# Two heads of layer 0 side by side on TensorE, with the softmax sums added up on GpSimd

## The chip, the cores and the metric

The kernel runs on one core of a Trainium2 chip. A core has five engines that each work through a queue of their own in order: TensorE (PE; its weight loads are shown as PEld), VectorE (DVE), ScalarE (ACT), GpSimd (POOL) and SyncE (SP, which here issues DMAs). The metric is the device time of one execution in microseconds (us). Three runs of the kernel before gave 4607.11, 4602.47 and 4614.23 us, a median of 4607.11 us.

## The reference

Four layers are applied one after the other to four images of 32 x 32 pixels with 384 channels; every layer adds its result to its input. Only layer 0 is touched by the change. It is attention with six heads of 64 channels, in which each head's keys and values are sampled at moved positions and a sampled table of relative positions is added to the logits:

```python
k = (xs @ w_k + b_k).reshape(Bq, n, HEADS, HC)
v = (xs @ w_v + b_v).reshape(Bq, n, HEADS, HC)
attn = jnp.einsum('bmhc,bnhc->bhmn', qh, k) * scale
bias = _bilinear_sample(rpe_img, disp)
bias = bias.reshape(Bq, G, n, n, GH).transpose(0, 1, 4, 2, 3).reshape(Bq, HEADS, n, n)
attn = jax.nn.softmax(attn + bias, axis=-1)
out = jnp.einsum('bhmn,bnhc->bmhc', attn, v).reshape(Bq, Hq, Wq, NC)
return out @ w_out + b_out
```

Here n is 1024 (pixels), HEADS is 6 and HC is 64. So an image has six 1024 x 1024 logit matrices. Layers 1 to 3 (a second attention with twelve heads, a box filter, and a local attention) stay as they are.

## The kernel before, in words

All arithmetic is in float32. A channel chunk is 128 channels on 128 partitions, so three chunks (k = 0 to 2) hold the 384 channels, and each chunk holds two heads of 64 channels. Pixels are taken in eight blocks of 128 keys (j) and in two halves of 512 queries (q).

**Two lanes.** `Front` runs layer 0, `Trunk` runs layers 1 to 3. Layer 0 of image 0 runs alone, with a schedule of its own (`heads0`, L897 and after). Layer 0 of images 1, 2 and 3 is a generator that is advanced beside layers 1 to 3 of the image before it: each `yield w` of a lane states a share of the lane's work, and `Net.layer3` moves the front on until it is a little ahead of the trunk. That mixes the emission of the two lanes. The framework then reorders instructions on each engine within what the data and the buffers allow, so the order on an engine is its own and not that of the source; once built, each engine's order is fixed and a waiting instruction holds up those behind it.

**The stage around the change.** For each head h and query half q, `head0` (L815 to L895) does the following. For each j it has GpSimd gather a window of the position table (`win`, L830, an indirect DMA, four buffers), ScalarE and VectorE interpolate it (L842 and L847 on ScalarE, L843 and L848 on VectorE) into a logits tile `lg` of 128 keys x 512 queries (13 buffers), TensorE makes keys x queries in a PSUM bank (L851), and VectorE adds that to the logits (L852) and keeps a running maximum (L855, L857). The keys of one head lie in a tile `kz` of 128 partitions in which the other head's 64 rows are zero, so that the multiplication can run over the whole chunk. Then the maximum is turned on TensorE (L864), reduced (L868), spread over the partitions through a diagonal made on GpSimd (L870), a product with ones (L872) and a copy (L876). Last, for each j, VectorE subtracts it (L883), ScalarE takes the exponential (L884) and TensorE does two products of 64 output rows each (L886): the head's values, and a block of ones whose result is the softmax sum. Results and sums share one PSUM bank. `over_sums` (L1111) divides after each pair of heads: the sums go to DRAM and back for the reciprocals, which return spread over the partitions as two `inv` tiles.

**The trunk beside it.** In a pair of layer 1 heads (`pair`, six an image), a step j has TensorE make two logit tiles of two PSUM banks each (L1509), ScalarE take their exponentials (L1517), TensorE make the weights (transposes L1534, products L1539 of a tile `sg` that GpSimd scales at L1492) and VectorE multiply (L1546). Four products for the next pair's sums (L1382), their maximum on VectorE (L1390) and their exponentials on ScalarE (L1391) run in the same step, and so does the product with the values (L1481).

**PSUM.** Two tiles of two banks (`big`) and four tiles of one bank (`bank`) take all eight banks. Before, the front's stage uses only `bank`; the trunk's logits and sums go through `big`.

**DMA queues.** SP issues most loads and stores, among them the keys (L813) and the sums (L894). GpSimd's queue holds the window gathers L830, the scaling L1492 and the diagonal L870.

Of the kernel before, what the change touches and what calls it, by code (L numbers as in the profile page):

```python
# [26 lines left out]
P = 128  # L27
# [45 lines left out]
class Net:  # L73
# [132 lines left out]
    def scratch(self):  # L206
# [13 lines left out]
        self.k0 = dram("k0", [C, N])  # L220
        self.gcd = dram("gcd", [C, M1])
# [204 lines left out]
class Front(Lane):  # L426


    def layer0(self, b):
        nc, v = self.nc, self.nc.vector  # L430
        with self.scope("l0"):
# [3 lines left out]
            self.kz = [self.wt([P, N], f"kz{r}") for r in range(2)]  # L435
            for r in range(2):
                nc.gpsimd.memset(self.kz[r][GC * (1 - r) : GC * (2 - r), :], 0.0)
            self.va = self.wt([P, NJ, C], "va")
            self.f = self.wt([P, 2, 2, NJ * G], "bias_f")
            self.widx = self.wt([P, 2, NJ * G], "widx", 1, I32)  # L440
            if b == 0:

                self.side = "left"
                with self.scope("l0f"):
                    self.side = "right"
                    self.heads = self.heads0(self.work)
                    with self.scope("l0a"):
                        yield from self.inputs0(b)
                    yield from self.heads
                    self.side = "left"  # L450
                    yield from self.outputs0(b)
                    self.side = "right"
                return
            with self.scope("l0a"):
                yield from self.inputs0(b)
            with self.scope("l0b"):
                self.load_keys(0)
                for h in range(G):
                    if h + 1 < G:
                        self.load_keys(h + 1)  # L460
                    for q in range(2):
                        yield from self.head0(h, q)
                    if h % 2:
                        yield from self.over_sums(h // 2)
# [166 lines left out]
    def inputs0(self, b):  # L631
# [145 lines left out]
        va, bv = self.va, self.rows[:, R_BV0 : R_BV0 + C]  # L777
# [3 lines left out]
        def value(j):  # L781
            v.tensor_tensor(va[:, j, :], self.dense_n(xsT, w, j), bv, ALU.add)
# [32 lines left out]
    def head0(self, h, q):  # L815

        nc, v = self.nc, self.nc.vector
        f, kz, va = self.f, self.kz[h % 2], self.va
        k, r0 = h // 2, (h % 2) * GC
        rows = slice(r0, r0 + GC)  # L820
        other = slice(GC - r0, 2 * GC - r0)
        HH, HN = HW // 2, N // 2
        both = self.qpad[:, k, 1 + HH * q : 1 + HH * (q + 1), 1 : 1 + HW]
        queries = both[rows]
        logits = []
        rmax = self.wt([P, HN], "rmax", 2)
        for j in range(NJ):
            c = j * G + h
            win = self.wt([P, (HH + 1) * WROW], "win", 4)
            nc.gpsimd.indirect_dma_start(  # L830
                out=win,
                out_offset=None,
                in_=self.strips[:, :],
                in_offset=bass.IndirectOffsetOnAxis(
                    ap=self.widx[:, q, c : c + 1], axis=0
                ),
            )
            wv = win.rearrange("p (r c) -> p r c", c=WROW)
            sc = lambda i, t: f[:, i, t, c : c + 1]

            z = self.wt([P, HH, HW + 1], "z", 3)
            nc.scalar.activation(z, wv[:, 0:HH, 0 : HW + 1], AF.Copy, scale=sc(1, 1))  # L842
            v.scalar_tensor_tensor(  # L843
                z, wv[:, 1 : HH + 1, 0 : HW + 1], sc(0, 1), z, ALU.mult, ALU.add
            )
            lg = self.wt([P, HH, HW], "lg", 13)
            nc.scalar.activation(lg, z[:, :, 0:HW], AF.Copy, scale=sc(1, 0))  # L847
            v.scalar_tensor_tensor(lg, z[:, :, 1 : HW + 1], sc(0, 0), lg, ALU.mult, ALU.add)  # L848
            lf = lg.rearrange("p y x -> p (y x)")
            ps = self.bank()  # L850
            nc.tensor.matmul(ps, kz[:, j * P : (j + 1) * P], both, start=True, stop=True)  # L851
            v.tensor_tensor(lf, ps, lf, ALU.add)  # L852
            logits.append(lf)
            if j == 1:
                v.tensor_tensor(rmax, logits[0], lf, ALU.max)  # L855
            elif j > 1:
                v.tensor_tensor(rmax, rmax, lf, ALU.max)  # L857
            yield 3


        NI = HN // P
        ps = self.bank()
        for i in range(NI):
            nc.tensor.transpose(  # L864
                ps[:, i * P : (i + 1) * P], rmax[:, i * P : (i + 1) * P], self.ident
            )
        top = self.wt([P, NI], "top", 2)
        v.tensor_reduce(top, ps.rearrange("p (i n) -> p i n", i=NI), AX.X, ALU.max)  # L868
        diag = self.wt([P, NI, P], "diag", 1)
        nc.gpsimd.tensor_tensor(diag, bc(self.ident, 1, NI), bc(top, 2, P), ALU.mult)  # L870
        ps = self.bank()
        nc.tensor.matmul(  # L872
            ps, self.ones, diag.rearrange("p i n -> p (i n)"), start=True, stop=True
        )
        tb = self.wt([P, HN], "tb", 2)
        nc.scalar.copy(tb, ps)  # L876
        yield 3


        po = self.bank()  # L880
        for j in range(NJ):
            lf = logits[j]
            v.tensor_tensor(lf, lf, tb, ALU.subtract)  # L883
            nc.scalar.activation(lf, lf, AF.Exp)  # L884
            for out, w in ((rows, va[:, j, h * GC : (h + 1) * GC]), (other, self.ones[:, 0:GC])):
                nc.tensor.matmul(po[out, :], w, lf, start=j == 0, stop=j == NJ - 1)  # L886
            if j % 2:
                yield 2

        nc.scalar.copy(queries, po[rows, :].rearrange("p (y x) -> p y x", y=HH))  # L890
        o0 = other.start
        den = logits[0][o0 : o0 + 1, :]
# [1034 lines left out]
```

## Time and profile before

| what | value |
|---|---|
| median of the three runs | 4607.11 us |
| span of the profiled execution (first to last instruction) | 4578.1 us |
| median less span | 29.0 us |
| TensorE busy | 4150.6 us, 91% of the span |
| VectorE busy | 3138.6 us, 69% |
| ScalarE busy | 2303.6 us, 50% |
| GpSimd busy | 972.6 us, 21% |
| mean granted TensorE clock | 0.948 of full speed |

The profile gives no other time for its execution than the span; what lies around it is taken as the 29.0 us between that and the median. A group in the profile has one line per source line, engine, operation and tile: how many records, their busy time together, the mean of one, and the idle time before them with what ended it. A float32 product of 512 columns leaves two records on TensorE, so 288 instructions show as 576. Overlapping records are counted once in busy time. In a timeline the first two columns are the start and the length in us; "x8" merges eight records.

### The profile page before, as it was taken

Reading aid. Unit: us, or ns where it says so; the run is one execution under the profiler, and the core shown is the slowest. Engines: PE = TensorE matmul, PEld = TensorE weight load, DVE = VectorE, ACT = ScalarE, POOL = GpSimd, SP = SyncE. Lnnn points to the kernel's source line nnn. Section 1 sums busy time; section 2 is a strip of 40 time slices with the busy share of each in tenths; the row PEclk is TensorE's granted clock in tenths of the full one; section 3 lists DMA queues with packets and bytes.
Section 4 is the critical chain, followed back from the end, with each engine's and each line's share of the span. In section 5 each row is a group of like instructions: output and inputs, shape, how many; then the busy total and the mean of one; then the engine's idle time right before and its main releaser. Section 6 shows DMA issues by size and latency. Waiting matters only on the chain.

```text
span 4578.1 us, 47313 instructions
## 1 busy us (share of the span) xinstructions
PE 4150.6 (91%) x15896; PEld 1795.0 (39%) x15896; DVE 3138.6 (69%) x5909; ACT 2303.6 (50%) x3633; POOL 972.6 (21%) x994
## 2 busy tenths in 40 slices
PE   5699889999999898999999989899999998999998
PEld 2333334333334443433333444343333335344444
DVE  4599466878787628687878744678786884566654
ACT  2266334667664314465666422456665641555632
POOL 1644123212111104211212110522120211000000
PEclk8799989999999898999999989899999998999998
DMA  6444234212121245321212134432121213311011
GB/s 139 150 144 129 79 125 123 64 52 84 51 59 55 86 114 164 93 55 39 84 50 79 38 105 125 135 103 66 45 71 36 72 38 123 105 32 27 20 41 42
DMA packets 232852, 371.01 MB, mean 81 GB/s; under 512 B 117763, under 2 KB 165728, under 8 KB 232608
## 3 DMA queue, kind: packets, MB, share of 16 engines
q1 hardware_dynamic: 180568, 201.26, 15.4%
q0 software_dynamic: 39936, 145.53, 10.8%
q10 hardware_dynamic: 12104, 21.19, 1.4%
q8 instruction: 126, 2.06, 0.2%
q14 instruction: 118, 0.97, 0.1%
HBM read 287.90 MB, written 80.27 MB: 80 GB/s over the span
## 4 chain that ended last, share of the span: by engine, by line
PE 56%; DVE 14%; ACT 7%; issue 5%; DMA 4%; POOL 2%; SPq 0%; ACTq 0%; DVEq 0%; POOLq 0%
PE bank L1539 13%; PE big L1509 5%; PE big L1382 4%; PE bank L851 4%; PE big L403 4%; PE bank L886 4%; PE bank L417 4%; PE bank L1534 3%; PE bank L1481 3%; DVE nmax L1390 2%; DVE e L1546 2%; PE bank L1219 2%; PE big L666 2%; PE big L1664 1%; POOL gat L738 1%
## 5 line engine op out<-in xcount | busy, mean ns | idle before, releaser
L1539 PE MATMUL bank<-whole,sg 128*128 128x512 f32 (+3 forms) x2304 | 852.5, 505 | 7.0 <-POOL sg L1492 7.0
L1546 DVE SCALAR_TENSOR_TENSOR e<-bank,gam,e 128x512 f32<-128x512 f32 x768 | 561.9, 747 | 349.2 <-PE bank L1539 226.7
L1391 ACT ACTIVATE big<-big,nmax 128x1024 f32<-128x1024 f32 x384 | 417.6, 1087 | 322.3 <-DVE nmax L1390 322.1
L1517 ACT ACTIVATE e<-big 128x1024 f32<-128x1024 f32 x384 | 379.7, 1019 | 363.2 <-PE big L1509 362.1
L1539 PEld LDWEIGHTS bank<-whole,sg 128*128 128x128 f32 x2304 | 403.4, 197 | 369.6 <-issue 281.6
L1390 DVE TENSOR_REDUCE nmax<-big 128x1 f32<-128x1024 f32 x384 | 454.5, 1219 | 76.4 <-PE big L1382 75.9
L830 POOL DMA_INDIRECT win<-strips,widx x288 | 316.2, 1098 | 658.0 <-DVE z L843 391.8
L1492 POOL TENSOR_SCALAR sg<-whole,gam 128x512 f32<-128x512 f32 x192 | 143.7, 750 | 1442.6 <-PE bank L1539 1019.6
L1509 PE MATMUL big<-qa,ka 64*128 64x512 f32 x1536 | 417.8, 630 | 9.7 <-ACT big L1391 9.5
L1382 PE MATMUL big<-k,q 32*128 32x512 f32 x1536 | 327.7, 674 | 82.2 <-ACT big L1391 45.2
L738 POOL DMA_INDIRECT gat<-pairs,sidx x192 | 209.2, 1090 | 378.8 <-DVE ix_gt L519 217.4
L851 PE MATMUL bank<-qpad,kz 128*128 128x512 f32 x576 | 278.8, 613 | 9.4 <-ACT gf L1551 9.4
L886 PE MATMUL bank<-lg,va 128*64 128x512 f32 x576 | 265.6, 605 | 15.0 <-ACT lg L884 14.9
L886 PE MATMUL bank<-lg,ones 128*64 128x512 f32 x576 | 265.0, 605 | 0.0
L848 DVE SCALAR_TENSOR_TENSOR lg<-z,bias_f,lg 128x512 f32<-128x512 f32 x288 | 213.7, 759 | 47.4 <-ACT lg L847 45.7
L1509 PEld LDWEIGHTS big<-qa,ka 64*128 64x128 f32 x1536 | 135.7, 188 | 256.3 <-issue 124.3
L842 ACT ACTIVATE z<-win,bias_f 128x528 f32<-128x528 f32 x288 | 202.9, 735 | 55.4 <-DVE lg L848 34.4
L852 DVE TENSOR_TENSOR lg<-bank,lg 128x512 f32<-128x512 f32 x288 | 192.9, 685 | 49.4 <-PE bank L851 48.1
L883 DVE TENSOR_TENSOR lg<-lg,tb 128x512 f32<-128x512 f32 x288 | 191.5, 710 | 46.9 <-ACT tb L876 46.9
L843 DVE SCALAR_TENSOR_TENSOR z<-win,bias_f,z 128x528 f32<-128x528 f32 x288 | 215.5, 772 | 11.3 <-ACT z L842 9.8
L1481 PE MATMUL bank<-e,vs 128*32 128x512 f32 x1536 | 206.7, 604 | 3.9 <-DVE vs L1475 3.9
L847 ACT ACTIVATE lg<-z,bias_f 128x512 f32<-128x512 f32 x288 | 200.0, 716 | 12.0 <-PE bank L886 6.1
(314 smaller groups left out, 6620.8 us busy)
## 6 DMA issues: line engine op xcount, KB each, us to landing
pairs<-xn SPq DMA_DIRECT2D x64, 192.0 KB
q<-qd SPq DMA_DIRECT2D x48, 256.0 KB
w<-in_gmat SPq DMA_DIRECT2D x16, 576.0 KB
w<-in_w_off SPq DMA_DIRECT2D x12, 576.0 KB
w<-in_Wqkv SPq DMA_DIRECT2D x12, 576.0 KB
a<-in_x SPq DMA_DIRECT2D x16, 384.0 KB
x<-a ACTq DMA_DIRECT2D x4, 1536.0 KB
res<-x SPq DMA_DIRECT2D x12, 512.0 KB
```

Of the source, the lines that this page charges most:

```text
L738: nc.gpsimd.indirect_dma_start(out=gat[:, g].rearrange("p l c -> p (l c)"), out_offset=None, in_=pairs[:, :], in_offset=bass.IndirectOffse ...
L830: nc.gpsimd.indirect_dma_start(out=win, out_offset=None, in_=self.strips[:, :], in_offset=bass.IndirectOffsetOnAxis(ap=self.widx[:, q, c : ...
L851: nc.tensor.matmul(ps, kz[:, j * P : (j + 1) * P], both, start=True, stop=True)
L886: nc.tensor.matmul(po[out, :], w, lf, start=j == 0, stop=j == NJ - 1)
L1382: nc.tensor.matmul(ps[r][:, h * 512 : (h + 1) * 512], self.q4[rows, i * P : (i + 1) * P], self.k4[rows, 0:512], start=True, stop=True,)
L1390: v.tensor_reduce(nmax[:, r, i : i + 1], ps[r], AX.X, ALU.max, negate=True)
L1391: nc.scalar.activation(ps[r], ps[r], AF.Exp, bias=nmax[:, r, i : i + 1], accum_out=den[:, r, i : i + 1],)
L1481: nc.tensor.matmul(av[r0 : r0 + HD1, :], vs[:, r, :], es[h][:, r, :], start=j == 0, stop=j == NJ - 1,)
L1509: nc.tensor.matmul(ps[:, r, :], ka[rows, j * P : (j + 1) * P], qa[rows, cols], start=True, stop=True,)
L1517: nc.scalar.activation(e, ps, AF.Exp)
L1539: nc.tensor.matmul(ps[:, (mid - i0) * P :], sg[:, r, m, :], sim[:, h, r, m, (mid - i0) * P :], start=m == 0, stop=m == 1,)
L1546: v.scalar_tensor_tensor(e[:, r, :], ps, self.gam[:, 1:2], e[:, r, :], ALU.add, ALU.mult, accum_out=tot[:, r, h : h + 1],)
```

## The change

In images 1 to 3 the two heads of a chunk are now one unit (`two_heads`, six an image, in place of twelve calls of `head0`).

- The keys of a chunk are one tile of 128 partitions (`keys`, one buffer), 64 partitions a head; the two products of a j use 64 partitions each and write the two halves of a `big` tile. `kz` stays in image 0 alone.
- The values are written to a DRAM tensor `v0` (L782 before wrote them into `va` in SBUF) and loaded per chunk (`vals`, one buffer).
- Logits tiles are 128 x 1024 (two heads), nine buffers, so the additions, maxima, subtractions and exponentials are half as many and twice as wide. The interpolation keeps its size.
- The two products with the values write 64 partitions each of one bank. The product with ones in every j is gone: GpSimd adds up the exponential tiles (seven additions of 128 x 1024 a unit), and two products with ones follow at the end of the unit.
- The turned maxima and the product that spreads them go through `big` tiles; the diagonal is made in two parts.
- The `inv` tiles use the tag `z` (three buffers) in place of `lg`; the layer 1 tile `y` uses the tag `sg`.

```diff
+    def pair_keys(self, k):
+        t = self.wt([P, N], "keys")
+        self.nc.sync.dma_start(t, self.k0[k * P : (k + 1) * P, :])
+        return t
+    def pair_values(self, k):
+        t = self.wt([P, NJ, P], "vals")
+        self.nc.sync.dma_start(
+            t, self.v0[:, k * P : (k + 1) * P].rearrange("(j p) c -> p j c", p=P)
+        )
+        return t
-    def head0(self, h, q):
+    def two_heads(self, k, q):
...
         for j in range(NJ):
-            ps = self.bank()
-            nc.tensor.matmul(ps, kz[:, j * P : (j + 1) * P], both, start=True, stop=True)
-            v.tensor_tensor(lf, ps, lf, ALU.add)
+            lg = self.wt([P, 2, HN], "lg", 9)
+            ps = self.big()
+            for r in range(2):
+                nc.tensor.matmul(
+                    ps[:, r * HN : (r + 1) * HN],
+                    keys[half(r), j * P : (j + 1) * P],
+                    queries[half(r)],
+                    start=True,
+                    stop=True,
+                )
...
+            v.tensor_tensor(flat(lg), ps, flat(lg), ALU.add)
...
         po = self.bank()
+        acc = self.wt([P, 2, HN], "rmax", 2)
         for j in range(NJ):
-            v.tensor_tensor(lf, lf, tb, ALU.subtract)
-            nc.scalar.activation(lf, lf, AF.Exp)
-            for out, w in ((rows, va[:, j, h * GC : (h + 1) * GC]), (other, self.ones[:, 0:GC])):
-                nc.tensor.matmul(po[out, :], w, lf, start=j == 0, stop=j == NJ - 1)
+            lg = logits[j]
+            v.tensor_tensor(flat(lg), flat(lg), tb, ALU.subtract)
+            nc.scalar.activation(flat(lg), flat(lg), AF.Exp)
+            for r in range(2):
+                nc.tensor.matmul(
+                    po[half(r), :], vals[:, j, half(r)], lg[:, r], start=j == 0, stop=j == NJ - 1
+                )
+            if j:
+                first = logits[0] if j == 1 else acc
+                nc.gpsimd.tensor_tensor(flat(acc), flat(first), flat(lg), ALU.add)
...
+        ps = self.bank()
+        for r in range(2):
+            nc.tensor.matmul(
+                ps[half(r), :], self.ones[:, 0:GC], acc[:, r], start=True, stop=True
+            )
...
-            inv = self.wt([P, HH, HW], "lg", 13)
+            inv = self.wt([P, HH, HW], "z", 3)
```

The steps that the units state with `yield` add up to 76 a unit, as two calls of `head0` did.

## The prediction

> **What bounds the kernel now.** I first looked at busy time by engine: TensorE is busy 91% of the span. Then I asked where the changed lines run. They lie between 820 and 3769 us, in three stretches, one for each of images 1 to 3, in which layer 0 of an image shares the core with layers 1 and 2 of the image before. The view of busy time by stretch gives these stretches, and then one pair of layer 1 heads with the front beside it (975 to 1098) and one without (4124 to 4204):
>
> ```profile
> core 0: us, PE busy (x) PEld busy (x) DVE busy (x) ACT busy (x) POOL busy (x), PEclk, DMA share, GB/s
> 820.00:1541.00 721.00, 676.66 (x2632) 272.17 (x2631) 575.24 (x1097) 441.04 (x685) 136.51 (x136) 0.98 0.20 56
> 1933.00:2654.00 721.00, 676.86 (x2633) 272.17 (x2632) 575.83 (x1097) 441.41 (x685) 136.39 (x136) 0.98 0.20 56
> 3045.00:3769.00 724.00, 678.92 (x2636) 273.95 (x2635) 576.78 (x1097) 441.43 (x686) 137.30 (x137) 0.98 0.19 56
> ...
> 975.00:1098.00 123.00, 113.77 (x473) 45.05 (x469) 94.57 (x188) 77.59 (x124) 19.39 (x21) 1.00 0.17 47
> ...
> 4124.00:4204.00 80.00, 77.87 (x364) 33.46 (x363) 50.05 (x116) 48.20 (x76) 5.53 (x8) 1.00 0.12 28
> ```
>
> In each stretch TensorE is 94% busy (676.7 of 721), VectorE 80% (575.2), ScalarE 61%, GpSimd 19%. TensorE is the bound, and VectorE is not far behind. The front costs a pair 43 us (123 less 80): 36 us of TensorE and 44.5 us of VectorE.
>
> The groups show what the change takes from TensorE, and the rows of which VectorE's new operations are made:
>
> ```profile
> L851 PE MATMUL bank<-qpad,kz 128*128 128x512 f32 x576 | 278.8, 613 | 9.4 <-ACT gf L1551 9.4
> L886 PE MATMUL bank<-lg,va 128*64 128x512 f32 x576 | 265.6, 605 | 15.0 <-ACT lg L884 14.9
> L886 PE MATMUL bank<-lg,ones 128*64 128x512 f32 x576 | 265.0, 605 | 0.0
> L852 DVE TENSOR_TENSOR lg<-bank,lg 128x512 f32<-128x512 f32 x288 | 192.9, 685 | 49.4 <-PE bank L851 48.1
> L883 DVE TENSOR_TENSOR lg<-lg,tb 128x512 f32<-128x512 f32 x288 | 191.5, 710 | 46.9 <-ACT tb L876 46.9
> ```
>
> Mean durations on TensorE overlap, so starts must be compared. TensorE's timeline:
>
> ```profile
> 1179.69 0.59 PE L886 MATMUL bank<-lg,va 128*64 128x512 f32 x1
> 1179.69 0.59 PE L886 MATMUL bank<-lg,ones 128*64 128x512 f32 x1
> 1180.12 0.59 PE L886 MATMUL bank<-lg,va 128*64 128x512 f32 x1
> ...
> 1199.82 1.99 PE L851 MATMUL bank<-qpad,kz 128*128 128x512 f32 x4
> 1201.74 1.99 PE L1509 MATMUL big<-qa,ka 64*128 64x512 f32 x8
> 1203.66 1.09 PE L1534 MATMUL bank<-ident,gf 128*128 128x128 f32 x8
> ```
>
> The two 64-column products of L886 start together, and the next two 0.43 us later: they already run side by side, so one head's values and sums cost 2 x 0.43 = 0.86 us a block. Two products of L851 take 1.92 us, 0.96 each. L1509, 64 rows deep like the new keys product, gets four products into the same 1.92 us: they run in pairs, 0.96 a pair.
>
> **The change, part by part** (per image, a third of the whole; six units, 96 head blocks, 48 new blocks of two heads).
>
> *TensorE.* Keys: L851 is 278.8 / 3 = 92.9 us; after, 48 x 0.96 = 46.1. Saved 46.8. Values: 96 x 0.86 = 82.6; after, 48 x 0.86 = 41.3. Saved 41.3. Added: the two products with ones, 6 x 0.86 = 5.2. Turning and spreading the maximum keeps its count (8 transposes and 2 products a unit). So 676.7 becomes 593.8, 249 us less over three images.
>
> *VectorE.* The row nearest to a 128x1024 operation is L1691 at 1.23 us (both inputs in SBUF), or L1684 at 1.22 (one in PSUM). Two narrow ones cost 1.34 (192.9 / 144), 1.33 (191.5 / 144) and 1.37 (maximum, 0.687 each). 48 x (0.12 + 0.10) + 42 x 0.14 = 16.4 saved: 575.2 becomes 559. ScalarE saves about 10 and stays far from a bound.
>
> *GpSimd.* It gets 42 additions of 128x1024. The nearest row is L1686, a 128x1024 addition of 2.408 us: 101 us, so 136.5 becomes 238 of 721. That alone is no bound. [...] The trace has one clean meeting of the two:
>
> ```profile
> 1525.43 1.22 DVE L1684 SCALAR_TENSOR_TENSOR dn<-big,sq 128x1024 f32<-128x1024 f32 x1
> 1526.57 4.16 DVE L883 TENSOR_TENSOR lg<-lg,tb 128x512 f32<-128x512 f32 x5
> ...
> 1525.31 2.45 POOL L1686 TENSOR_TENSOR whole<-sq,whole 128x1024 f32<-128x1024 f32 x1 [3.74 <-ACT sq L1680]
> ```
>
> L1684, with one input in PSUM, ran its usual 1.22 us under the addition. The five subtractions after it, both inputs in SBUF, took 4.16 us where back-to-back starts of 0.61 make 3.1: about 1.05 us of the addition's 2.45, or 43%, came out of VectorE. [...] It falls where it hurts: the additions follow the exponentials, so VectorE then has the remaining wide subtractions in its queue, later the interpolation (L843, L848) of the next unit, all with two SBUF inputs; only the trunk's L1546 and L1390, which read PSUM, can lie under an addition. I take the row, 43, because those two (4 x 0.75 + 2 x 1.22) make up some 5 of each 10 us of trunk step, and keep 0 and 101 as ends.
>
> *What the sum makes of it.* Neither engine's work alone gives the time, since each waits for the other: before, 721 us stand over 676.7 + 575.2 = 1251.9 us of both, a factor of 0.576. I keep that factor, which credits a microsecond off TensorE with 0.58. After: 593.8 + 559 + 43 = 1196, times 0.576 = 689, 32 less an image, **97 less in all** (0 on VectorE instead of 43: 171 less; 101: 4 more).
>
> *New waits.* (1) The keys products now take the `big` tiles that L1509 needs next. Behind a keys product on TensorE stand L1509, the transposes and L1382; L1509 must wait until VectorE has added the previous product (1.22 us, after the small divisions L1472 to L1475, 0.17 + 0.16 + 0.25). Before, it did not. Some 5 steps a unit have two such products, and the second product (0.96) and transposes (about 1 us) stand against it. 1.22 + 0.58 less 0.96 and half the transposes leaves 0.3 a step, so I take 1.5 a unit, times 18 units = 27; the ends are 0 (all transposes ahead) and 4 (none). (2) The products with ones wait on TensorE for the last GpSimd addition, with the next L1509 behind them: 0 to 2.4 us a unit, taken 0.5, 9 in all. (3) The two `inv` tiles hold two of three `z` buffers for the way to DRAM and back (sums copied at 1057.4, product done at 1068.8: 11 us). The next unit's interpolation stands still then, six times in all; VectorE has trunk work meanwhile: 0 to 5 us each, taken 1, 6 in all. Together 42, ends 0 and 145.
>
> *Costed at nothing.* The diagonal's two halves keep 1.04 us each. SP gets 24 value stores, 9 key and 9 value loads for 18 key loads, 24 more issues of about 0.5 us. The value stores share the two `xn` buffers: a store has about 3.9 us (two of L417's steps, 15.5 us for eight) where the existing waits for such stores are 2.5 us (22.3 / 9). Uncovered, 6 x 2.5 x 3 = 45 us. The loads of keys and values are issued a phase ahead (22 of a unit's 76 shares of 123 us, 36 us); their cover is that phase, and a late load would cost its own few us six times. `y` in the `sg` ring delays one scaling a pair by its store, against a 10 us step. The `kz` clearing goes (0.95 us each, idle engine).
>
> Sum: -97 + 42 = -55. On the profile's own time 4578 becomes 4523; with the 29 us around it, 4552.
>
> **Rivals.** [...] *VectorE isn't held at all*: -171 + 42, 4478. For it: GpSimd may find VectorE in its PSUM work. *TensorE alone decides*: 593.8 at the 94% of before is 632, 89 less an image, 4340; against it, VectorE would have to be 95% busy. *The products don't pair*: the keys saving is lost, +140 x 0.576 = +81, 4633; the 64-row pairs of L1509 speak against it (2%).
>
> **How the numbers follow.** A measurement of this kernel can tell about 0.3%, 14 us, from no change. The likeliest case, a partial gain of 15 to 95 us (4510 to 4592), 35%; VectorE not held, 12%; TensorE alone, 3%: faster 50%. Within 14 us, 11%. Slower 39%: GpSimd 27%, the new waits at their upper ends 10%, no pairing 2%. I predict 4552. The range takes in the slower rival and VectorE unheld: 4455 to 4680.
>
> **What would show it.** The keys group with 64x512 records starting in pairs 0.96 apart, and TensorE busy near 594 in a stretch. The GpSimd additions at 2.4 us; longer means that they wait. VectorE subtractions well over 1.23 us are the price of meeting, 1.05 us an addition by my sum. L1509 waiting for the logits addition, 1.5 us a unit. If VectorE's busy time passes 640 in a stretch, or TensorE idles over 120, the forecast is wrong.

## The result and the profile after

| | before | after |
|---|---|---|
| median of four runs side by side | 4610.67 us | 4756.86 us |
| ratio (95% interval) | | 1.0328 (1.0294 to 1.0361) |
| span of the profiled execution | 4578.1 us | 4743.7 us |
| TensorE busy | 4150.6 us | 4057.8 us |
| VectorE busy | 3138.6 us | 3267.9 us |
| GpSimd busy | 972.6 us | 1351.4 us |
| mean granted TensorE clock | 0.948 | 0.917 |

The change costs 146 us where I forecast a gain of 55, and the time lies above the range. The view of busy time by stretch, over image 1's layer 0, which now takes until about 1588 us:

```profile
core 0: us, PE busy (x) PEld busy (x) DVE busy (x) ACT busy (x) POOL busy (x), PEclk, DMA share, GB/s
820.00:1588.00 768.00, 641.55 (x2474) 251.86 (x2471) 619.69 (x963) 427.52 (x621) 269.41 (x183) 0.92 0.20 55
```

VectorE's 620 us are near the 602 of my sum. TensorE is busy 642 us instead of 594. The clock explains most of that: while TensorE was busy, the lowered clock took 46 us from it, against 15 in the same stretch before, so 31 of the 48 us; the other 17 are products that took longer than my sum has them. TensorE also idles 126 us, against 44 before. Neither engine has become busier than TensorE was; both wait. Two groups of the kernel before, then the groups after:

```profile
L1509 PE MATMUL big<-qa,ka 64*128 64x512 f32 x1536 | 417.8, 630 | 9.7 <-ACT big L1391 9.5
L848 DVE SCALAR_TENSOR_TENSOR lg<-z,bias_f,lg 128x512 f32<-128x512 f32 x288 | 213.7, 759 | 47.4 <-ACT lg L847 45.7
```

```profile
L844 PE MATMUL big<-qpad,keys 64*128 64x512 f32 x576 | 159.0, 646 | 17.5 <-ACT big L1439 13.9 <-ACT whole L1485 3.6
L1557 PE MATMUL big<-qa,ka 64*128 64x512 f32 x1536 | 462.2, 658 | 109.0 <-DVE lg L875 72.9 <-ACT e L1565 20.4 <-ACT big L1439 14.5
L926 POOL TENSOR_TENSOR rmax<-rmax,lg 128x1024 f32<-128x1024 f32 x108 | 319.6, 2960 | 31.5 <-ACT lg L919 24.9
L918 DVE TENSOR_TENSOR lg<-lg,tb 128x1024 f32<-128x1024 f32 x144 | 252.6, 1784 | 106.3 <-ACT tb L910 106.3
L872 DVE SCALAR_TENSOR_TENSOR lg<-z,bias_f,lg 128x512 f32<-128x512 f32 x288 | 252.9, 892 | 12.0 <-ACT lg L871 10.5 <-ACT e L1565 1.4
L896 POOL TENSOR_TENSOR diag<-ident,top 128x512 f32<-128x512 f32 x36 | 37.4, 1039 | 154.1 <-issue 90.9 <-DVE top L892 37.7 <-PE big L902 25.6
```

L844 is the new keys product: 159 us for what took 278.8 (L851). L1557, layer 1's keys product (L1509 before), had 9.7 us of idle time before it and now has 109, of which 72.9 end with the logits addition L875. L926 are the additions, 2.96 us each instead of 2.41. L918, the wide subtraction, takes 1.78 us instead of 1.23, and the interpolation L872 (L848 before) 892 ns instead of 759. L918 also waits 106.3 us for the spread maximum, where the two narrow ones waited 46.9.

**Where 166 us of span went.** Split each span into three: TensorE idle; TensorE busy, but its time lost because the granted clock was under full speed (its busy time, each part weighted with one less the clock); and the rest, TensorE's work at full speed. The experiments' splits stand here too, for use below:

| us | idle | lost to the clock while busy | work at full speed |
|---|---|---|---|
| before | 427 | 175 | 3976 |
| after | 686 | 269 | 3788 |
| e1, no sums | 546 | 248 | 3777 |
| e5, no sums, single tiles | 471 | 245 | 3807 |
| e6, sums on TensorE | 545 | 229 | 3892 |
| e10, before, with the additions | 539 | 251 | 3981 |
| e13, before, with waits | 493 | 258 | 3989 |

So TensorE's work fell by 188 us, three quarters of the 249 of the forecast. But its idle time grew by 259 and its loss to the clock by some 94: -188 + 259 + 94 = 165. Nearly all the new idle time is in long waits: between TensorE's first and last instruction, waits of 2 us or more rose from 44 (216 us together) to 108 (473 us).

One caution on "before": every later run lists time and span of the same execution, and they differ by 2 to 4 us. So the 29 us between the median and the span of the profile before are not time around the program; its profiled execution was some 27 us faster than its median (clock 0.948, and 0.940 to 0.946 in the runs beside the experiments). Differences of spans against it are too large by about that: 166 us of span stand for 146 us of time.

One of the long waits, in the timeline of the three engines and then in windows of 4 us:

```profile
1184.18 1.21 DVE L918 TENSOR_TENSOR lg<-lg,tb 128x1024 f32<-128x1024 f32 x1
...
1185.39 3.30 DVE L918 TENSOR_TENSOR lg<-lg,tb 128x1024 f32<-128x1024 f32 x1
1188.62 2.40 DVE L1523 TENSOR_TENSOR vs<-vp,rt 128x64 f32<-128x64 f32 x1
...
1192.07 8.34 DVE L872 SCALAR_TENSOR_TENSOR lg<-z,bias_f,lg 128x512 f32<-128x512 f32 x3
1200.33 0.74 DVE L1594 SCALAR_TENSOR_TENSOR e<-bank,gam,e 128x512 f32<-128x512 f32 x1
...
1184.29 15.57 POOL L926 TENSOR_TENSOR rmax<-rmax,lg 128x1024 f32<-128x1024 f32 x5 [2.32 <-ACT lg L919]
...
1201.13 3.78 PE L1587 MATMUL bank<-whole,sg 128*128 128x512 f32 x4 [5.79 <-DVE e L1594]
```

```profile
core 0: us, PE busy (x) PEld busy (x) DVE busy (x) ACT busy (x) POOL busy (x), PEclk, DMA share, GB/s
...
1192.00:1196.00 4.00, 1.61 (x8) 0.31 (x6) 4.00 (x3) 2.71 (x3) 3.92 (x2) 0.98 0.00 0
1196.00:1200.00 4.00, 0.00 (x0) 0.00 (x0) 4.00 (x2) 0.74 (x1) 3.78 (x2) 0.50 0.01 2
1200.00:1204.00 4.00, 2.87 (x4) 1.31 (x5) 4.00 (x8) 2.19 (x3) 1.29 (x1) 0.50 0.02 4
1204.00:1208.00 4.00, 4.00 (x14) 1.20 (x12) 4.00 (x9) 3.66 (x7) 1.60 (x3) 0.74 0.52 157
1208.00:1212.00 4.00, 4.00 (x22) 1.29 (x20) 4.00 (x11) 3.77 (x7) 2.12 (x3) 1.00 0.19 59
```

Five additions stand in a row on GpSimd for 15.57 us, and five VectorE instructions are held, one for each: a subtraction takes 3.30 us instead of 1.21, a small trunk product (L1523, 128x64) 2.40 instead of 0.22, three interpolations of 0.74 us take 8.34. Together that is some 10 us. Behind them stands L1594, trunk work that reads PSUM: what it needs was done by 1194.15 us (L1582's product at 1190.99, L1565's exponential last), it ran its 0.74 us from 1200.33 on, and TensorE waits for it: 5.79 us idle. When it starts again its clock is 0.50, and it is back at full speed only some 5 us later. VectorE shows as fully busy throughout, although it is being held.

### The profile page after: what moved, and what is told of

Same layout as the page of the kernel before. It is cut to its first block, busy times and chain, and to the rows that moved or that the text cites. A ratio compares the mean times of both kernels' runs of the same rounds, so it can differ in the third digit from the quotient of the medians.

```text
span 4743.7 us, 45840 instructions
## 1 busy us (share of the span) xinstructions
PE 4057.8 (86%) x15392; PEld 1733.1 (37%) x15392; DVE 3267.9 (69%) x5477; ACT 2272.5 (48%) x3438; POOL 1351.4 (28%) x1114
## 5 line engine op out<-in xcount | busy, mean ns | idle before, releaser
L1587 PE MATMUL bank<-whole,sg 128*128 128x512 f32 (+3 forms) x2304 | 891.7, 520 | 43.7 <-DVE e L1594 36.7
L1594 DVE SCALAR_TENSOR_TENSOR e<-bank,gam,e 128x512 f32<-128x512 f32 x768 | 562.0, 747 | 342.0 <-PE bank L1587 230.4
L1557 PE MATMUL big<-qa,ka 64*128 64x512 f32 x1536 | 462.2, 658 | 109.0 <-DVE lg L875 72.9
L1540 POOL TENSOR_SCALAR sg<-whole,gam 128x512 f32<-128x512 f32 x192 | 169.5, 883 | 1320.6 <-PE bank L1587 710.9
L1438 DVE TENSOR_REDUCE nmax<-big 128x1 f32<-128x1024 f32 x384 | 453.7, 1218 | 98.8 <-PE big L1430 82.0
L1565 ACT ACTIVATE e<-big 128x1024 f32<-128x1024 f32 x384 | 383.8, 1018 | 286.1 <-PE big L1557 284.5
L926 POOL TENSOR_TENSOR rmax<-rmax,lg 128x1024 f32<-128x1024 f32 x108 | 319.6, 2960 | 31.5 <-ACT lg L919 24.9
L918 DVE TENSOR_TENSOR lg<-lg,tb 128x1024 f32<-128x1024 f32 x144 | 252.6, 1784 | 106.3 <-ACT tb L910 106.3
L1557 PEld LDWEIGHTS big<-qa,ka 64*128 64x128 f32 x1536 | 139.0, 193 | 387.3 <-DVE lg L875 150.7
L872 DVE SCALAR_TENSOR_TENSOR lg<-z,bias_f,lg 128x512 f32<-128x512 f32 x288 | 252.9, 892 | 12.0 <-ACT lg L871 10.5
L919 ACT ACTIVATE lg<-lg 128x1024 f32<-128x1024 f32 x144 | 149.6, 1053 | 90.0 <-DVE lg L918 88.7
L1599 ACT COPY gn<-bank 128x128 f32<-128x128 f32 (+2 forms) x288 | 104.7, 369 | 181.2 <-DVE e L1594 181.0
L1430 PEld LDWEIGHTS big<-k,q 32*128 32x128 f32 x1536 | 94.8, 193 | 259.1 <-ACT e L1565 108.8
```

The lines of the kernel that those rows point to most:

```text
L872: v.scalar_tensor_tensor(lr, z[:, :, 1 : HW + 1], sc(0, 0), lr, ALU.mult, ALU.add)
L918: v.tensor_tensor(flat(lg), flat(lg), tb, ALU.subtract)
L926: nc.gpsimd.tensor_tensor(flat(acc), flat(first), flat(lg), ALU.add)
L1430: nc.tensor.matmul(ps[r][:, h * 512 : (h + 1) * 512], self.q4[rows, i * P : (i + 1) * P], self.k4[rows, 0:512], start=True, stop=True,)
L1438: v.tensor_reduce(nmax[:, r, i : i + 1], ps[r], AX.X, ALU.max, negate=True)
L1557: nc.tensor.matmul(ps[:, r, :], ka[rows, j * P : (j + 1) * P], qa[rows, cols], start=True, stop=True,)
```

## The experiments

Each batch ran beside the kernel before, whose median went from 4581 to 4611 us between batches; so ratios to it are compared, and 0.1% is 4.6 us.

**The sums left out, and moved (e1, e2).** e1 takes the GpSimd addition away, and the product with ones reads the last exponential tile, so the softmax sums are left out:

```diff
-        acc = self.wt([P, 2, HN], "rmax", 2)
+        acc = logits[NJ - 1]
-            if j:
-                first = logits[0] if j == 1 else acc
-                nc.gpsimd.tensor_tensor(flat(acc), flat(first), flat(lg), ALU.add)
```

> The changed kernel without its 126 GpSimd additions; the product with ones reads the last exponential tile, so the softmax sums are left out of the computation. Holding theory (the additions keep VectorE from its two-input instructions): the wide subtractions fall from 1.78 to 1.23 us and the interpolation back to 0.76 and 0.77, 126 us of VectorE are given back and most of it reaches the time: 4600 to 4650 us. PSUM theory (layer 1's logits products wait for the two-bank tiles of the front): the additions matter only through what they add to that wait, 4690 to 4720 us, with the wait at L1557 for the logits addition still about 70 us. Queue theory (the additions stand in GpSimd's queue ahead of the scaling and the gathers): as low as the holding theory; the memset run tells these two apart.

Measured: 0.993 (0.9899 to 0.9961). So the additions cost 1.0328 - 0.993 = 4.0%, some 185 us, and all the rest of the change together gains 0.7%, some 32 us. The page's line of busy time in e1:

```profile
PE 4025.5 (88%) x15392; PEld 1730.8 (38%) x15392; DVE 3074.1 (67%) x5477; ACT 2264.2 (50%) x3438; POOL 981.6 (21%) x988
```

VectorE has the same instructions in both kernels, and is busy 3267.9 us with the additions on GpSimd and 3074.1 without: they hold it for 194 us, 1.54 us each. e2 makes the same 126 additions on VectorE:

```diff
-                nc.gpsimd.tensor_tensor(flat(acc), flat(first), flat(lg), ALU.add)
+                v.tensor_tensor(flat(acc), flat(first), flat(lg), ALU.add)
```

> The changed kernel with the same 126 additions of 128x1024 on VectorE instead of GpSimd, 1.23 us each, 155 us on VectorE in all. Holding theory: GpSimd's additions took 126 us from VectorE anyway, and 2.4 us each in which it couldn't be chosen when; the time stays within 40 us of the changed kernel, 4720 to 4790 us, and the subtractions fall to 1.23 us. Queue theory: taking the additions out of GpSimd's queue helps more than VectorE's 155 us cost, 4690 us or less. If VectorE were not a bound at all, the run would be at 4640.

Measured: 1.014 (1.0098 to 1.0182). The additions take 1.22 us there, the subtractions are back at 1.22, and VectorE is busy 3204.8 us instead of 3267.9: VectorE is busy for less time when it does the additions itself than when GpSimd does them.

**GpSimd writes in the place of the additions (e4).** Each addition is replaced by five GpSimd writes of 128x512; the sums are left out:

```diff
-                nc.gpsimd.tensor_tensor(flat(acc), flat(first), flat(lg), ALU.add)
+                for part in range(5):
+                    nc.gpsimd.memset(spare[:, part % 2], 0.0)
```

> The changed kernel with each GpSimd addition replaced by five 128x512 memsets on GpSimd, which only write (about as long as the addition, by the 0.95 us of a 64x1024 memset); the softmax sums are left out of the computation as in the run without sums. Holding theory: an instruction that reads nothing from SBUF doesn't hold VectorE, so the subtractions are at 1.23 us and the time is that of the run without sums within 20 us, 4600 to 4660 us. Queue theory: GpSimd is as busy as in the changed kernel, so the time stays near it, 4730 to 4760 us.

Measured: 1.0138 (1.0102 to 1.0173). The groups:

```profile
L927 POOL MEMSET rmax<- 128x512 f32 x630 | 303.3, 538 | 3.5
...
L919 DVE TENSOR_TENSOR lg<-lg,tb 128x1024 f32<-128x1024 f32 x144 | 171.0, 1219 | 108.2 <-ACT tb L910 108.2
```

The subtractions are not held (1.219 us), and yet 2.4 us of writes per addition's place cost 2.1% over e1. VectorE is held elsewhere. The trunk's cast L1457, of 128x16 elements, has a median of 175 ns in e1; here it takes 1940 ns on average, and up to 8.07 us under a row of writes, with a TensorE product behind it:

```profile
L1457 DVE CAST dsum<-den 128x16 f32<-128x16 int32 x24 | 46.6, 1940 | 5.6 <-ACT big L1440 5.5
...
2371.66 8.49 POOL L927 MEMSET rmax<- 128x512 f32 x18
2372.11 8.07 DVE L1457 CAST dsum<-den 128x16 f32<-128x16 int32 x1
...
2382.36 0.38 PE L1465 MATMUL bank<-ident,dsum 128*16 128x128 f32 x1 [9.63 <-DVE dsum L1463]
```

TensorE's waits at L1465 came to 62.0 us, 19.1 at the same place in e1: 43 of the 64 us that it idles more than there. The writes wait for nothing and so run ahead, and the window gathers come late behind them as well: ScalarE waited 51.7 us for windows, 28.4 in e1. So this run doesn't show what an occupied queue costs without a hold, and neither theory stands as it was written. The changed kernel's own trace says more of the queue. With the additions in it, ScalarE's waits for windows are 32.7 us instead of 28.4, and TensorE's for the tiles that GpSimd scales 6.9 instead of 6.7. Waits of ScalarE that end with an addition come to 7.0. So the queue's share in the 185 us is small, and the hold is the rest.

**The additions alone (e10).** The kernel before, with 252 additions of 128x512 that nobody reads:

```diff
             nc.scalar.activation(lf, lf, AF.Exp)
+            if j == 0:
+                acc = self.wt([P, HN], "rmax", 2)
+            else:
+                nc.gpsimd.tensor_tensor(acc, logits[0] if j == 1 else acc, lf, ALU.add)
```

> The kernel before, with the additions alone: each exponential tile of 128x512 is also added up on GpSimd, 84 x 3 additions that nobody reads; the sums still come from TensorE. By my forecast's price (half of 1.05 us of VectorE each, times 0.576): 252 x 0.52 x 0.576 = +76 us, ratio 1.016. Theory A (in runs of additions VectorE gets one instruction through per addition, TensorE then waits and its clock falls): +100 to +190 us, ratio 1.022 to 1.04, TensorE waits over 2 us at least twice as many as before. Theory C (additions do harm only beside the wide tiles and the one long chain of the changed kernel): +0 to +40 us, ratio under 1.01.

Measured: 1.0396 (1.0367 to 1.0424), 187 us between the medians, the same price as in the changed kernel; theory C falls. The groups:

```profile
L888 POOL TENSOR_TENSOR rmax<-rmax,lg 128x512 f32<-128x512 f32 x216 | 333.4, 1543 | 51.4 <-ACT lg L884 38.1
...
L883 DVE TENSOR_TENSOR lg<-lg,tb 128x512 f32<-128x512 f32 x288 | 319.6, 1154 | 46.1 <-ACT tb L876 46.1
```

The subtractions grew from 710 to 1154 ns, 128 us in all. With the other instructions that are held, VectorE is busy 3333.3 us instead of 3138.6: 195 us over 252 additions, 0.77 each, where the forecast's half was 0.52. 195 us of hold became 187 us of time, 0.96 for one, not 0.576. In the split, TensorE's idle time grew by 112 us and its loss to the clock by 76. Waits of 2 us or more rose from 44 to 68, short of the doubling expected.

**Shorter turns (e12).** Each addition is cut in two of 128x512.

```diff
-                nc.gpsimd.tensor_tensor(flat(acc), flat(first), flat(lg), ALU.add)
+                for r in range(2):
+                    nc.gpsimd.tensor_tensor(acc[:, r], first[:, r], lg[:, r], ALU.add)
```

> The changed kernel with every addition on GpSimd cut in two of 128x512. Theory A (in a run of additions VectorE and GpSimd take turns, one whole instruction each, so that shorter additions let VectorE's instructions through twice as often): 40 to 80 us less than the changed kernel, 4680 to 4720 us, VectorE's 128x1024 subtraction under 1.6 us (1.78 in the changed kernel). Rival (VectorE loses in proportion to what GpSimd reads): the same within 15 us, ratio to before 1.03, subtraction 1.75 or more.

Measured: 1.0273 (1.0246 to 1.0301), subtractions 1.62 us. VectorE is busy 39 us less than in the changed kernel (3229.3). The direction is that of the turns, the gain (0.55%, 25 us) less than the 40 to 80 us that I expected, and the intervals overlap: it supports the reading weakly.

**A wait by itself (e11, e13).** Can a wait cost more than its length? In the kernel before, the product that spreads the maximum was made to wait for GpSimd writes:

```diff
+        fresh = self.wt([P, P], "fresh", 1)
+        for _ in range(12):
+            nc.gpsimd.memset(fresh, 1.0)
         nc.tensor.matmul(
-            ps, self.ones, diag.rearrange("p i n -> p (i n)"), start=True, stop=True
+            ps, fresh, diag.rearrange("p i n -> p (i n)"), start=True, stop=True
```

> The kernel before, and nothing but waits: in each of the 36 units of a head chain (12 an image) the product that spreads the maximum takes a tile of ones that GpSimd writes anew by 12 writes of 128x128 (about 0.2 us each, 2.46 together) after the diagonal. [...] If a microsecond of TensorE's waiting costs at most itself: up to 36 x 2.46 = +89 us, ratio 1.019 or less. Theory A (a wait over 2 us also halves the granted clock for some us after it, 2 to 3.5 us lost each): +140 to +200 us, ratio 1.03 to 1.044, and the clock's loss between 820 and 3800 us, 131 us before, at 200 or more. Rival: other work catches up in part, +50 us or less.

Measured: 0.9998 (0.9986 to 1.0011). The run tests nothing: the writes depend on nothing, so the framework placed them right after the previous unit's product (at 925.58 us, 0.1 us after it), and no wait arose. In e13, VectorE first copies the reduced maximum into `fresh` (`v.tensor_copy(fresh[:, 0:NI], top)`), so that the writes must follow.

> The kernel before, again with nothing but waits: the tile of ones for the product that spreads the maximum is now first touched by VectorE with the head's own reduced maximum (8 bytes a column, under 0.1 us), so that GpSimd's 12 writes (0.206 us each, 2.5 together) can't run ahead as they did in the run before, and must stand behind the reduction. If a microsecond of TensorE's waiting costs at most itself: +89 us at most, ratio 1.019 or less. Theory A (a wait over 2 us also halves the granted clock for some us, 2 to 3.5 us lost each): the trace shows about 30 waits over 2 us more than before, the clock's loss between 820 and 3800 us rises from 131 to 200 us or more, and the time by 140 to 200 us, ratio 1.03 to 1.044. Rival (the queues of TensorE hold enough to catch up): +50 us or less, ratio under 1.011.

Measured: 1.0314 (1.0292 to 1.0336), 141 us between the medians. The waits of TensorE, one of them in the timeline, and the windows around it:

```profile
PE bank L876 <- POOL fresh L875: 63.8, 33, 3.7
```

```profile
1066.14 3.08 POOL L875 MEMSET fresh<- 128x128 f32 x12
...
1069.28 2.08 PE L876 MATMUL bank<-diag,fresh 128*128 128x512 f32 x2 [1.78 <-POOL fresh L875]
```

```profile
1064.00:1068.00 4.00, 3.44 (x12) 0.89 (x10) 3.38 (x4) 1.35 (x2) 2.50 (x9) 1.00 0.00 0
1068.00:1072.00 4.00, 2.72 (x7) 1.58 (x8) 0.77 (x1) 1.50 (x4) 0.99 (x5) 0.58 0.00 0
1072.00:1076.00 4.00, 4.00 (x10) 2.21 (x10) 2.72 (x6) 2.31 (x4) 0.00 (x0) 0.56 0.00 0
1076.00:1080.00 4.00, 4.00 (x19) 1.10 (x19) 3.56 (x8) 2.39 (x5) 0.69 (x1) 1.00 0.00 0
```

33 waits of 1.9 us, 63.8 us together, cost 141. The split of the span says how: idle +66, loss to the clock +83, work +13. (Together that is 161 of span against 141 of time, for the reason given with the split.) After the wait of 1.78 us in the timeline the clock is halved for some 7 us. Of the expected signs, 28 waits over 2 us were new where I expected 30 (44 became 72). VectorE's copy was not the 0.1 us that I had put down, an estimate that no run shows (a copy of 128x4 in the kernel before, L132, took 0.163), but 0.715 us, 25.7 in all, at the time of GpSimd's diagonal: perhaps a hold of its own, which I don't separate. If all of it reached the time, 115 us would be left for the 64 us of waits, still 1.8 for one.

**The shared wide tile (e3, e5).** The keys products go into two single PSUM tiles, added by two narrow additions (e5 leaves the sums out as well):

```diff
-            ps = self.big()
+            ps = [self.bank() for _ in range(2)]
...
-            v.tensor_tensor(flat(lg), ps, flat(lg), ALU.add)
+            for r in range(2):
+                v.tensor_tensor(lg[:, r], ps[r], lg[:, r], ALU.add)
```

> The changed kernel with the two keys products of a block in two single PSUM banks instead of one two-bank tile, and the logits addition in two narrow halves (144 x 0.12 = 17 us more on VectorE). PSUM theory: the wait at L1557 for the logits addition (73 us of TensorE idle) goes, and the time falls to 4660 to 4690 us. Holding theory: VectorE is what is late, and the wait moves to the transposes and products L1582 and L1587 that need single banks: 4730 to 4770 us.

> Leaves out the softmax sums (the product with ones reads the last exponential tile) and puts each keys product into its own single PSUM tile, added by two narrow additions, as before the change. Theory A (the shared wide PSUM tile is a cost of its own, about 30 us as in the run that gave the changed kernel single tiles, and adds to that of the GpSimd additions): 4570 - 30 = 4540 us, the wait of layer 1's keys product on VectorE (68 us without sums) nearly gone. Theory B (that wait only takes the place of other idle time of TensorE once GpSimd no longer holds VectorE): 4560 to 4575, as without sums alone.

Measured: e3 1.0274 (1.0238 to 1.0309), e5 0.9853 (0.9836 to 0.9871). In e3 the group of layer 1's keys product:

```profile
L1558 PE MATMUL big<-qa,ka 64*128 64x512 f32 x1536 | 460.3, 638 | 18.3 <-ACT big L1440 17.8 <-ACT whole L1486 0.2
```

The wait for the logits addition is gone (109.0 to 18.3 us of idle time), and the time falls by 0.5% with GpSimd's sums and 0.8% without, though the keys products then pair less well (229 us instead of 159; 160 of the 288 pairs start together, all 288 in the wide tile). Theory A of e5 holds: new wait (1) costs some 25 to 35 us in these two.

**The sums on TensorE (e6, e7).** The keys stay side by side, but values and sums go head after head, as before the change; e7 adds the single tiles. The core of the edit:

```diff
+    def head_products(self, po, r, j, lg):
+        own, other = slice(r * GC, (r + 1) * GC), slice((1 - r) * GC, (2 - r) * GC)
+        for out, w in ((own, self.vals[:, j, own]), (other, self.ones[:, 0:GC])):
+            self.nc.tensor.matmul(po[out, :], w, lg[:, r], start=j == 0, stop=j == NJ - 1)
...
+        for j in range(NJ):
+            self.head_products(po, 1, j, logits[j])
```

> Keeps the keys products of two heads side by side, but sums and values go head after head on TensorE, as before the change; no additions on GpSimd or VectorE. TensorE gets 3 x 41 us of products back, less 16 us for the products with ones that go. My forecast's factor (0.576 of the work of both engines) puts it at 4570 + 0.576 x 108 = 4632 us. Theory A (without the sums TensorE is no longer the bound: it idles between VectorE's and ScalarE's steps, and runs at a lower granted clock, so that products put into its gaps cost little): 4575 to 4600 us, granted clock over 0.93.

> As the kernel with the sums on TensorE, head after head, and in addition single PSUM tiles for the keys products. Theory A: 20 to 30 us under that kernel, about 4550 to 4570 us, and so faster than the kernel before by about 1%. Theory B (the wide PSUM tile costs nothing of its own): the same as that kernel.

Measured: e6 1.0193 (1.0166 to 1.022), e7 1.0136 (1.0116 to 1.0157). My theory A for e6 falls: 108 us of products put back cost 2.6% over e1, 121 us, although TensorE idles 546 us in e1. By the split, e6 has 115 us more work than e1 and the same idle time: a microsecond of TensorE work put back costs about one. My edit issues the second head's 16 products in one go, which may be part of it. So e1's small gain (199 us less work than before, 32 us less time) doesn't show that TensorE's work is cheap. It points to costs that the change brings with it, sums or no sums: e1 idles 119 us more than the kernel before and loses 73 more to the clock.

**Towards a version that beats both (e8, e9, e14, e15).** e8 joins e2 and e3: additions on VectorE, single tiles. e9 moves half of the pause after the spread maximum to a place before the diagonals. e14 adds a second diagonal tile; to make room, the sums are added up in the first exponential tile. e15 uses that room for a tenth logit tile instead.

```diff
         v.tensor_reduce(top, ps.rearrange("p (i n) -> p i n", i=NI), AX.X, ALU.max)
+        yield 3
...
-            diag = self.wt([P, NI // 2, P], "diag", 1)
+            diag = self.wt([P, NI // 2, P], "diag", 2)
...
-        yield 6
+        yield 3
...
-        acc = self.wt([P, 2, HN], "rmax", 2)
+        acc = logits[0]
```

> The changed kernel with its 126 additions on VectorE, and single PSUM tiles for the keys products. If the 91 us that GpSimd's additions cost over VectorE's and the 30 us of the wide PSUM tile are separate and add: 4666 - 30 = 4636 us. If they are one thing (VectorE late for the logits additions): 4660 us.

> The changed kernel with its additions on VectorE and the keys products in single PSUM tiles (1.0015 of before), and one of the two pauses around the spreading of the maximum moved into it: after the reduction of the turned maximum the trunk gets 3 of the 6 shares, so that its products stand on TensorE between the transposes and the products of the diagonals. Theory A (what the change loses are long waits of TensorE, each paid again by some 3 us of half clock after it; this chain is one place of them, 21.5 us in waits for the diagonal): 20 to 45 us less than that kernel, ratio to before 0.992 to 0.997. Theory B (VectorE and ScalarE set the pace, TensorE's waits move elsewhere): unchanged within 10 us, ratio 1.000 to 1.003.

> The kernel with the additions on VectorE, single PSUM tiles and the pause in the chain, ratio 0.9983, with two diagonal tiles instead of one (room for it from adding the sums up in the first exponential tile). With one, the second multiply waited 1.26 us for the first product, 18 times, and ScalarE's copy and VectorE's subtractions behind it. Theory A (this serial chain is where part of the gain goes): 18 x 1.26 = 23 us less on the chain, 10 to 25 us less time, ratio 0.993 to 0.996. Rival (trunk work fills it): unchanged, ratio 0.997 to 1.000.

> The same kernel of ratio 0.9983 with one diagonal tile, but ten wide logit tiles instead of nine (room from the same place). Eight are held by a unit in its softmax, so one wide tile was left for running ahead, two heads' blocks, where the kernel before had five of 13. Theory A (the interpolation of the next unit stands still for want of a tile, and VectorE and ScalarE then wait for the chain): 15 to 40 us less, ratio 0.990 to 0.995. Rival (the pace is that of the trunk's requests): unchanged, 0.997 to 1.000.

Measured: e8 1.0015 (1.0001 to 1.0029), e9 0.9983 (0.9972 to 0.9994), e14 0.9917 (0.99 to 0.9933), e15 1.0025 (1.0012 to 1.0037). e8 is 1.25%, 57 us, under e2, twice the 30 us that single tiles gave elsewhere, so the two edits are not independent. e9 gains 0.3%, between its two theories. e14 gains 0.66% more, 30 us. The diagonal's and the subtraction's groups, e9 and then e14:

```profile
L898 POOL TENSOR_TENSOR diag<-ident,top 128x512 f32<-128x512 f32 x36 | 39.9, 1110 | 148.0 <-issue 77.4 <-PE big L904 36.5 <-DVE top L893 34.1
L920 DVE TENSOR_TENSOR lg<-lg,tb 128x1024 f32<-128x1024 f32 x144 | 174.7, 1239 | 85.3 <-ACT tb L912 85.3
```

```profile
L898 POOL TENSOR_TENSOR diag<-ident,top 128x512 f32<-128x512 f32 x36 | 42.3, 1196 | 115.1 <-DVE top L893 115.1
L920 DVE TENSOR_TENSOR lg<-lg,tb 128x1024 f32<-128x1024 f32 x144 | 176.4, 1247 | 65.7 <-ACT tb L912 65.7
```

The second multiply's 36.5 us of waiting for the first product are gone, and VectorE waits 65.7 us for the spread maximum instead of 85.3. e15, which adds up in the first tile as e14 does, is 0.4% slower than e9, so nothing speaks for that as the source of e14's gain, and room for running ahead was not what was short. e14 is 0.8% faster than the kernel before and 4% faster than the changed one.

## Why the prediction was wrong, step by step

In short: the forecast put the additions at 0.576 x 129 = 74 us and everything else at -129 (-171 and +42). The runs have 185 and -32. Two steps failed, the price of VectorE's hold and what the rest of the change makes of TensorE's time.

**The meeting was misread.** "[...] about 1.05 us of the addition's 2.45, or 43%, came out of VectorE." The five subtractions of that line are one record in the merged view. The first of them by itself:

```profile
1526.57 1.75 DVE L883 TENSOR_TENSOR lg<-lg,tb 128x512 f32<-128x512 f32 x1
```

It came when the addition (1525.31 to 1527.76) had run for half its time under L1684, which reads PSUM, and ended only after the addition; the next took 0.68 us, as usual. The 1.05 us are all that was left of the addition, not a part of its grip. So this row shows a hold up to the addition's end, and the turns above agree with it (a subtraction of 3.30 us instead of 1.21). Over all additions the hold is 1.54 us of 2.41, 194 us instead of 129, because much of VectorE's work reads PSUM and is not held: L1594 takes 747 ns, L1438 1218 and L875 1216 with the additions (no single one over 759, 1245 and 1227), and 747, 1218 and 1215 without (e1). No run shows the full 2.41 us at every addition, for which the forecast's end of 101 us an image and the slower rival's 27% stand: that is too much, the 1.05 too little.

**The price of the hold: the larger failure.** "I keep that factor, which credits a microsecond off TensorE with 0.58." The same factor put a microsecond of hold at 0.58. It cost 0.95 in the changed kernel (185 / 194) and 0.96 in the kernel before (e10), about the whole. Work that VectorE does itself cost less, 97 us for 131 us of busy time in e2, 0.74. An average over a stretch hides that the hold comes in runs of up to seven additions, in which everything behind it on VectorE stops and TensorE with it (5.79 us in the timeline above); that the runs make the difference to 0.74 is argued, and only weakly tested (e12). With 1.54 us in place of 1.05 and the factor kept, the sum would give 4589, still inside my range.

**TensorE's work: three quarters right.** 249 us less forecast, 188 found (199 in e1). The products do pair; four keys products (eight records) take as long as four of layer 1's:

```profile
1001.97 1.99 PE L844 MATMUL big<-qpad,keys 64*128 64x512 f32 x8
```

So the rival that they don't pair is out. But the keys products come to 148 us at full speed for the 138 of my sum, the products with the values to about 134 for 124, and layer 1's keys product takes about 23 us more than before.

**The clock: put at nothing.** I had the PEclk column in my first fence (0.98) and took it for fixed. In the kernel before, 25 of the 27 waits of 3 us or more were followed by a fall of the clock (over 1.5 us of busy time lost within 12 us), and 3.0 us were lost on average; of the 17 from 2 to 3 us, 12 were. After, it is 63 of 66, 2.8 us, and 35 of 42. Two waits close together share one fall, so more waits don't simply add up: the 64 new ones cost 94 us at most. With the wait of 5.79 us above the windows from 1196 to 1204 show 0.50, and in e13 one wait of 1.78 us went with 0.58 and 0.56 from 1068 to 1076. e13 shows that waits are a cause, not only company: 64 us of them cost 115 to 141. Of the change's 94 us, 73 are there in e1 without the additions, and 21 come with them; in the kernel before the additions alone bring 76.

**New wait (1): mis-sized.** 27 us forecast, 72.9 found, which is the upper end that I gave (4 a unit times 18); e3 and e5 put its worth at 25 to 35 us, e8 against e2 at 57. **(2)** didn't happen: no wait of TensorE on the last addition shows. **(3)** doesn't show either: VectorE waited 9.6 us for the reciprocals in `z`, and 18.3 before the change.

**Costed at nothing.** The value stores are free, as argued (steps of 1.93 us at 764 us, as before). The diagonal's halves are not: with one tile, the second multiply waits 1.26 us or more for the first product, and reduction, multiply, product, multiply, product and copy stand one behind another for 18 wide units; VectorE's wait for the spread maximum went from 46.9 to 106.3 us. I had looked at the durations of the halves and not at the buffer between them. e14 gives 30 us back by that.

**My signs.** TensorE idle over 120 us in a stretch came true (126); VectorE over 640 did not (620). The additions at 2.96 us and L918 at 1.784 were the signs of the hold that I had named.

**What stays open.** Why e5, with no sums at all and 169 us less TensorE work by the split, gains only 1.5%: its idle time is 44 us and its clock loss 70 us above before. The chain is part of it (e14), but how much is left, I can't tell. An e14 without sums was not tried. Nor do the runs show why the clock falls after some waits of 1 to 2 us (28 of 84 before, 14 of 57 after) and not after others.

## What to carry to other kernels

Before moving work to an idle engine, ask whom it holds while it runs, the small instructions of other stages too, and whether it comes in runs: a mean of 1.5 us per instruction, five times in a row, took 10 us from VectorE and left TensorE idle for 5.79. Unfold merged lines before reading a price from one. Convert work into time by the waits that it makes on the bounding engine, not by a fixed share of busy time, and look at that engine's clock after each wait: in the changed kernel a low clock followed 98 of the 108 waits of 2 us or more, and the 64 new ones cost up to 94 us by that, 1.5 each. When an operation is cut in two, check the buffers between the halves.

## What the runs showed of the hardware that I had not expected

- GpSimd's addition of 128x1024 takes 2.96 us under VectorE's load instead of 2.41: the turns cost both sides.
- What a held VectorE instruction lost did not go with its own size: in the timeline above a subtraction of 128x1024 lost 2.09 us, three interpolations of 128x512 2.04 each, and L1523 of 128x64 took 2.40 us instead of 0.22.
- GpSimd writes of 128x512 (538 ns each) leave VectorE's subtraction at 1.219 us, where the additions, which also read, put it at 1.784. But a cast of 128x16 under a row of 18 such writes took 8.07 us (e4).
- A TensorE wait of 1.78 us went with half clock for 6.8 us. Every stretch of half clock in the traces of before, after and e13 lasts a multiple of 3.41 us; there are 59, 93 and 90 of them.
- Two keys products in one wide PSUM tile start together every time (288 of 288); in two single ones they do 160 times.
